# The first batch's per-token maxima in groups of two hidden tiles instead of four, and three tiny range steps with two tensor operands

## The chip, the core and the metric

The kernel runs on one core of one Trainium2 chip. The metric is the device time of one execution in microseconds. The time before is the median of three runs. A separate execution was profiled: its span runs from the first to the last instruction of the program, and its own device time stands beside it in the table below.

## What is computed

`x` is (4, 1024, 512), `up_w` is (4096, 512), `down_w` is (512, 2048). Cut to what matters:

```python
scale = cond @ norm_w.T + 1.0
h = x * (scale[:, None, :] * rsqrt(mean(x * x) + EPS))
val, gate = split(h @ up_w.T, 2)          # 2048 + 2048 columns
h = val * gelu(gate)
s = 127.0 / max(|h| over the 2048 columns of a token)
hq = clip(round(h * s)) / s               # act_quant
y = hq @ weight_quant(down_w).T           # weights -1, 0, 1
out = y + x
```

The change touches two things in it. One is the maximum of |h| over the 2048 columns of each token, for the first of the four batches. The other is a step that the kernel adds for its own sake: each row of `up_w` is brought to a common range with a power of two before it is split in two float16 parts.

## The kernel before

**Tiling.** There are four batches of 1024 tokens. The 2048 hidden columns are 16 tiles of 128, numbered `j`, and each tile has the tokens in two halves of 512, called `h`. A finished tile of h (128 columns in the partitions, 2 x 512 tokens) lies in one slot of the ring `H`, which has 18 slots. In the first batch slots from 8 on also hold weights and staging until the tiles need them.

**The first batch.** `first_batch(j)` runs for j = 3 to 15 in an order written out by hand; nothing is scheduled by a planner there. For each j TensorE (PE) runs `plain_half(j, 0)` and `plain_half(j, 1)`: 12 matmuls for the gate into `pg` and 12 for the value into `pv`, of 512 tokens each (L588). ScalarE (ACT) applies gelu (L612), and VectorE (DVE) multiplies (L616), which writes the tile into its slot and frees the PSUM bank of `pv`. There are two such banks (tag "E"), so the value matmuls of one half wait for the L616 of two halves before.

Between the two halves every engine also prepares later work, and each takes its work in program order:

- *Weights of tile j+3.* `w_range` (called at the start of j) is four or five tiny DVE steps after one reduction: the largest value of a row (L279), its power of two (`pow2_floor`, L149), the scale factor (L285), the reciprocal (L288), and `w_gain` (L294). All but L279 work on a 128 x 2 tile. `w_scale` (ACT, L306) multiplies the weights, `w_rows` splits them in two parts (ACT L330, then DVE L331), and a transposing DMA (L332) puts them into place for PE.
- *Sums of weights for the later batches.* GpSimd (POOL) forms `s_sums` (L364 to L367) and `s_low` (L380), ACT `s_high` (L376), and SyncE (SP) writes them to DRAM.
- *Tokens of the second batch.* For j = 6, 8, 10, 12 DVE scales a group of tokens (`Tokens.scale`, L517), POOL forms four sums (L528 to L531), and in the following odd j ACT (L552) and DVE (L556) split them and SP transposes them (L559).
- *The largest value of each token.* `pair_max` reduces |h| over some slots. For the first group it writes the running maximum directly (L702); for each later one it reduces into a scratch tile `gm` (L707) and takes the maximum of the two (L709). The calls in the first batch are listed by j in the dictionary `LARGEST`; they stand right after `plain_half(j, 0)`, so the multiplication L616 of the second half and the token scaling L517 stand behind them on DVE. `D_SUM` and `TOKENS` are similar lists.

The pair of slots 14 and 15 is left for the start of the second batch. In batches two to four `pair_max` already takes two slots a call.

**Later batches.** From the second batch on `slot(g)` runs seven products of six matmuls per tile (L573) on sums of the weights and tokens, and the quantized product with `down_w` is spread over them. The two `Filler` queues decide there where DVE and ACT steps go. The code of those batches is not in the diff.

**Startup.** For j = 0 and 1 `w_range` runs before the first products, for j = 0 in two calls of 128 x 1 each. POOL scales (L308), PE transposes (L316), ACT and DVE split.

Of the kernel before, what the change touches and what calls it, by code (L numbers as in the profile page):

```python
# [8 lines left out]
F32 = mybir.dt.float32  # L9
# [3 lines left out]
I32 = mybir.dt.int32  # L13
AF = mybir.ActivationFunctionType
ALU = mybir.AluOpType
# [3 lines left out]
P = 128  # L19
EXPONENT = 0x7F800000  # L20
# [5 lines left out]
W_UP = 2.0**12  # L26
# [24 lines left out]
def glu_quant_kernel(  # L51
# [10 lines left out]
    PE, ACT, DVE, POOL, SP = nc.tensor, nc.scalar, nc.vector, nc.gpsimd, nc.sync  # L62
# [7 lines left out]
    NJ = FF // P  # L70
# [4 lines left out]
    cpool = ctx.enter_context(tc.tile_pool(name="const", bufs=1))  # L75
# [4 lines left out]
    ident = cpool.tile([P, P], F32, name="ident")  # L80
    neghalf = cpool.tile([P, 4], F32, name="neghalf")
    DVE.memset(neghalf, -0.5)
    unmagic = cpool.tile([P, 1], F32, name="unmagic")
    DVE.memset(unmagic, -MAGIC)
    one = cpool.tile([P, 1], F32, name="one")
# [38 lines left out]
    def m_view(b, h):  # L124
        return R[:, b % 2, M_AT + TOK * h : M_AT + TOK * (h + 1)]
# [16 lines left out]
    def h_slots(g, n=1):  # L142
        s = g % NSLOT
        return H[:, s : s + n]

    def pow2_floor(t):

        ti = t.bitcast(I32)
        DVE.tensor_scalar(ti, ti, EXPONENT, None, ALU.bitwise_and)  # L149

    def bank(tag, bufs, shape=None, name=None):
        return psum.tile(shape or [P, TOK], F32, name=name or tag, tag=tag, bufs=bufs)
# [6 lines left out]
    dx = cpool.tile([P, B], F32, name="dx")  # L159
# [58 lines left out]
    def cond_spread(dg, b0, b1, tag):  # L218
        n = b1 - b0
        pd = bank(tag, {"po": 3}.get(tag, 2), [P, B], f"pd_{b0}")[:, :n]  # L220
        PE.matmul(pd, ones[:n, :], dg, start=True, stop=True)
        return pd

    def cond_undo(pd, b0, b1):
        DVE.reciprocal(ux[:, b0:b1], pd)
        if b0 == 0:
            DVE.tensor_scalar(scT[:, :, 0], scT[:, :, 0], ux[:, 0:1], None, ALU.mult)
        DVE.tensor_copy(dx[:, b0:b1], pd)

    def cond_rows():  # L230

        pr = po_bank("pr", [NK * B, P])
        PE.transpose(pr, scT.rearrange("p k b -> p (k b)"), ident)
        rows = sm.tile([NK * B, P], F32, name="rows", bufs=1)
        DVE.tensor_copy(rows, pr)
        SP.dma_start(out=rows_dram, in_=rows)
# [14 lines left out]
    sw = cpool.tile([P, NJ, 2], F32, name="sw")  # L251
    sg0 = sm.tile([P, NJ, 2], F32, name="sg_0", tag="sg")
# [16 lines left out]
    def w_load(j, ts=(1, 0)):  # L269
        if j > 2:  # L270
            SP.dma_start(out=wn(j), in_=up_v[j])
            return
        for t in ts:
            SP.dma_start(out=wn(j)[:, t], in_=up_v[j][:, t])

    def w_largest(j, t0=0, t1=2):
        t = slice(t0, t1)
        am = sm.tile([P, 2], F32, name=f"wam_{j}_{t0}", tag="wam")[:, t]
        DVE.tensor_reduce(am, wn(j)[:, t], AX.X, ALU.max, apply_absolute_value=True)  # L279
        return am  # L280

    def w_factor(j, am, t0=0, t1=2):
        t = slice(t0, t1)
        pow2_floor(am)
        DVE.tensor_scalar(sw[:, j, t], am, 2.0**-100, 1.0 / W_UP, ALU.max, ALU.mult)  # L285
        if j not in iv:
            iv[j] = sm.tile([P, 2], F32, name=f"iv_{j}", tag="iv", bufs=3)
        DVE.reciprocal(iv[j][:, t], sw[:, j, t])  # L288

    def w_range(j, t0=0, t1=2):  # L290
        w_factor(j, w_largest(j, t0, t1), t0, t1)

    def w_gain(j):
        DVE.tensor_scalar(sg0[:, j, :], sw[:, j, :], dx[:, 0:1], None, ALU.mult)  # L294

# [3 lines left out]
    def w_scale(j, ts=(1, 0), eng=None):  # L301
        eng = eng or (ACT if j >= ROWS else POOL)
        for t in ts:
            w, r = wn(j)[:, t], iv[j][:, t : t + 1]
            if eng is ACT:
                ACT.activation(w, w, AF.Copy, scale=r)  # L306
            else:
                eng.tensor_scalar(w, w, r, 1.0, ALU.mult, ALU.mult)  # L308
# [49 lines left out]
    def s_sums(j):  # L358
        if j >= ROWS:
            v = wn(j).rearrange("p t (n f) -> p t n f", n=2)  # L360
            a11, a12, a21, a22 = v[:, 1, 0], v[:, 1, 1], v[:, 0, 0], v[:, 0, 1]
        else:
            a11, a12, a21, a22 = (wf(j)[:, n] for n in range(4))
        POOL.tensor_tensor(sf[:, 0], a21, a22, ALU.add)  # L364
        POOL.tensor_tensor(sf[:, 2], a11, a21, ALU.subtract)
        POOL.tensor_tensor(sf[:, 1], sf[:, 0], a11, ALU.subtract)
        POOL.tensor_tensor(sf[:, 3], a12, sf[:, 1], ALU.subtract)  # L367
# [6 lines left out]
    def s_high(j):  # L374
        for s, f in s_parts(j):
            ACT.copy(s[:, :, 0], f)  # L376
# [60 lines left out]
    def d_total():  # L437
        part = sm.tile([P, 1], F32, name="wpart", bufs=1)
        DVE.tensor_reduce(part, wsum, AX.X, ALU.add)
        return part  # L440
# [7 lines left out]
    def d_round(n):  # L448

        dn = d_part(n)  # L450
        ACT.activation(dn, dn, AF.Copy, scale=wsc, bias=MAGIC)
# [156 lines left out]
    def plain_half(j, h, between=nothing):  # L608
        pg = bank(*(("A", 2) if h or j == 1 else ("B", 1)), name=f"pg_{j}_{h}")
        plain(j, 1, h, pg)  # L610
        t1 = wpool.tile([P, TOK], F32, name=f"g_{j}_{h}", tag="t1")
        ACT.activation(t1, pg, AF.Gelu, scale=gain(j, 1))  # L612
        between()
        pv = bank("E", 2, name=f"pv_{j}_{h}")
        plain(j, 0, h, pv)
        DVE.scalar_tensor_tensor(h_half(j, h), pv, gain(j, 0), t1, ALU.mult, ALU.mult)  # L616
# [77 lines left out]
        z()  # L694


    def pair_max(b, i, h, pairs=1):

        v = h_slots(b * NJ + 2 * i, 2 * pairs)[:, :, h].rearrange("p j t -> p t j")
        m = m_view(b, h)  # L700
        if i == 0:
            return [lambda: DVE.tensor_reduce(m, v, AX.X, ALU.max, apply_absolute_value=True)]  # L702
        gm = []

        def largest():
            gm.append(wpool.tile([P, TOK], F32, name=f"gm_{b}_{i}_{h}", tag="gm", bufs=1))
            DVE.tensor_reduce(gm[0], v, AX.X, ALU.max, apply_absolute_value=True)  # L707

        return [largest, lambda: DVE.tensor_tensor(m, m, gm[0], ALU.max)]  # L709
# [260 lines left out]
    am = w_largest(0, 1, 2)  # L970
# [25 lines left out]
    def second_part():  # L996
# [12 lines left out]
    D_MEAN = 4  # L1009
    TOKENS = {6: 0, 8: 1, 10: 2, 12: 3}  # L1010
    LARGEST = {
        4: (0, 0, 2), 5: (0, 1, 2), 8: (2, 0, 2), 10: (2, 1, 2), 12: (4, 0, 2), 13: (4, 1, 2),
        14: (6, 0, 1), 15: (6, 1, 1),
    }
    toks = {}

    def next_tokens(j):

        if j in TOKENS:
            toks[j] = toks[j + 1] = Tokens(1, TOKENS[j])  # L1020
            toks[j].load()

    def s_all(j):
        s_high(j)
        s_low(j, POOL)
        s_spill(j)

    def first_batch(j, sc):

        if j + 2 <= LATE:  # L1030
            w_load(j + 4)
        if j >= 4:
            next_tokens(j + 2)
        t = toks.get(j)
        odd = t is not None and j not in TOKENS
        n = j + 2
        rows = LATE <= n < NJ
        if j + 1 < LATE:
            s_sums(j + 1)
        elif rows:  # L1040
            s_sums(n)
        if j + 3 < NJ:
            w_range(j + 3)
            w_gain(j + 3)
        if j == D_MEAN:
            part = d_total()
        plain_half(j, 0)
        if j == 3:
            pd = cond_spread(dg, 1, B, "po")
            cond_undo(pd, 1, B)  # L1050
            cond_rows()
        if j in LARGEST:
            for f in pair_max(0, *LARGEST[j]):
                f()
        if n < LATE:
            w_scale(n)
            w_rows(n)
        if j + 1 < LATE:
            s_all(j + 1)
        if t and not odd:  # L1060
            t.norm()
        for m in D_ROUND.get(j, ()):
            d_round(m)
            d_put(m)
        if t and not odd:
            t.scale(sc)
            t.sums()
        if j + 2 > LATE and j + 5 < NJ:
            w_load(j + 5)
        if odd:  # L1070
            t.high()
            t.low(DVE)
        if odd:
            t.turn()
        plain_half(j, 1)
        if j == D_MEAN:
            d_mean(part)
        own = rows and j + 1 >= LATE
        if own:
            s_high(n)  # L1080
            s_low(n, POOL)
        if LATE <= j + 3 < NJ:
            w_scale(j + 3)
            w_rows(j + 3)
        if own:
            s_spill(n)
        elif rows:
            s_sums(n)
            s_all(n)
            w_load(j + 5)  # L1090
        for n in D_SUM.get(j, ()):
            d_sum(n)
        if j in (NJ - 3, NJ - 1):
            s_load_x(NJ + (j - NJ + 3) // 2)
            s_load_y(NJ + (j - NJ + 3) // 2)
# [174 lines left out]
    for b in range(1, B):  # L1270
        dve, act = Filler(), Filler()
        gains(b)
        am = am_tile(b - 1)
        dq = state[b - 1] = sm.tile([P, 2 * NA], F32, name=f"dq_{b}", tag="dq")
        last_pair = NJ // 2 - 1
        for h in range(2):
            add_pair(
                dve, act, b - 1, last_pair, h, (0, "xz"[h]),
                lambda now, h=h: token_max(b - 1, h, am),
# [9 lines left out]
        pairs = {}  # L1289
# [111 lines left out]
    b = B - 1  # L1401
    am = am_tile(b)
# [158 lines left out]
```

## Time and profile before

| | us |
|---|---|
| median of 3 runs | 734.88 |
| the three runs | 734.56, 734.88, 737.32 |
| the profiled execution | 733.24 |
| its span | 731.4 |
| PE busy in the span | 720.9 |
| DVE busy | 587.2 |
| ACT busy | 396.1 |
| POOL busy | 195.8 |

The granted TensorE clock is 1.00 throughout. A matmul of 512 columns starts every 0.216 us where PE is not held up, so 12 of them take 2.59 us; the rows of the timeline show 2.75 us for 12, because the last one's own duration (0.379 us) overlaps the next. A gap of PE is therefore read from the starts: the start of a group minus the start of the one before, less 2.59 us. The page's idle times are smaller than these gaps by some 0.16 us each.

### The profile page before, as it was taken

The numbers are of one execution on the slowest core, as the hardware profiler recorded it, in microseconds if no ns is written. First come the engines' busy times: TensorE is split into PE (matmuls) and PEld (weight loads), VectorE is DVE, ScalarE is ACT, GpSimd is POOL, SyncE is SP. The second block draws the span as 40 slices with busy tenths as digits, with TensorE's granted clock in tenths as the row PEclk, the third lists the DMA queues.
The fourth block names the chain that finished last, engine by engine and source line by source line (L and its number), as shares of the span: only waits on it lengthen the run. The fifth ranks groups of instructions, "written<-read, shape, count | busy, mean of one in ns | idle before, by whom it ended". The sixth has DMA issues, their size and how long they took to land.

```text
span 731.4 us, 10126 instructions
## 1 busy us (share of the span) xinstructions
PE 720.9 (99%) x3661; PEld 358.9 (49%) x3661; DVE 587.2 (80%) x805; ACT 396.1 (54%) x629; POOL 195.8 (27%) x207
## 2 busy tenths in 40 slices
PE   7999999999999999999999999999999999999998
PEld 3544444444444446655444445665444444445744
DVE  6977889887498899797689887787678888755897
ACT  5868875872236675444335676543433665332274
POOL 1379886666200032450010030461020000000100
PEclk9999999999999999999999999999999999999999
DMA  6759998987544554886735646756934545452253
GB/s 233 252 165 307 291 286 233 254 199 180 165 94 106 134 121 147 191 164 172 194 100 102 130 101 173 187 146 165 226 98 106 91 100 115 103 103 90 87 189 115
DMA packets 203982, 117.30 MB, mean 160 GB/s; under 512 B 165382, under 2 KB 174487, under 8 KB 203932
## 3 DMA queue, kind: packets, MB, share of 16 engines
q1 hardware_dynamic: 203642, 116.33, 62.3%
q8 instruction: 28, 0.46, 0.3%
q10 hardware_dynamic: 290, 0.33, 0.2%
q14 instruction: 22, 0.18, 0.1%
HBM read 54.22 MB, written 23.09 MB: 106 GB/s over the span
## 4 chain that ended last, share of the span: by engine, by line
PE 87%; DVE 4%; POOL 4%; DMA 2%; ACT 1%; issue 1%; SPq 0%; POOLq 0%; DVEq 0%; ACTq 0%
PE A L573 34%; PE E L573 17%; PE B L573 8%; PE po L844 8%; PE pg L588 6%; PE pv L588 6%; PE po_end L793 4%; DVE gm L707 1%; PE po L793 1%; DMA H<-in_x_dram 1%; POOL xt L529 1%; DMA SXY<-H 1%; POOL H L367 1%; PE po_B L844 0%; POOL R L380 0%
## 5 line engine op out<-in xcount | busy, mean ns | idle before, releaser
L573 PEld LDWEIGHTS <-SXY 128*128 128x128 f16 x2016 | 197.3, 98 | 232.3 <-issue 0.6
L573 PE MATMUL A<-R,SXY 128*128 128x512 f16 x1152 | 266.3, 379 | 0.0
L573 PE MATMUL E<-R,SXY 128*128 128x512 f16 x576 | 140.0, 379 | 0.1
L671 DVE SCALAR_TENSOR_TENSOR H<-A,sg,t 128x512 f32<-128x512 f32 x48 | 36.0, 750 | 73.3 <-PE A L573 73.1
L588 PEld LDWEIGHTS <-SXY 128*128 128x128 f16 x486 | 47.4, 98 | 59.0 <-issue 1.7
L765 DVE TENSOR_TENSOR H<-H,am 128x1024 f32<-128x1024 f32 x64 | 76.2, 1216 | 0.0
L723 POOL PARTITION_ALL_REDUCE am<-R x8 | 14.3, 1793 | 230.4 <-DVE R L709 230.4
L684 ACT ACTIVATE t<-t,sg 128x512 f32<-128x512 f32 x48 | 34.6, 721 | 70.3 <-DVE t L681 70.2
L707 DVE TENSOR_REDUCE gm<-H 128x512 f32<-128x1024 f32 (+1 forms) x50 | 71.6, 1433 | 0.8
L573 PE MATMUL B<-R,SXY 128*128 128x512 f16 x288 | 70.0, 379 | 0.0
L588 PE MATMUL pg<-R,SXY 128*128 128x512 f16 x252 | 57.8, 379 | 0.3 <-DMA SXY<-H 0.3
L844 PE MATMUL po<-wd,R 128*128 128x256 fp8e4 (+1 forms) x448 | 56.8, 275 | 0.0
L588 PE MATMUL pv<-R,SXY 128*128 128x512 f16 x234 | 54.4, 379 | 1.1 <-DVE H L616 1.0
L844 PEld LDWEIGHTS <-R 128*128 128x128 bf16 (+1 forms) x480 | 47.0, 98 | 12.8
L668 ACT ACTIVATE t<-B,sg 128x512 f32<-128x512 f32 x48 | 33.0, 687 | 36.5 <-PE B L573 36.5
L477 POOL TENSOR_SCALAR ssq<-ssq 128x2 f32<-128x2 f32 x12 | 3.6, 298 | 176.8 <-ACT xt L507 124.1
L651 ACT COPY t<-A 128x512 f32<-128x512 f32 x48 | 27.9, 582 | 39.5 <-PE A L573 39.2
L659 ACT COPY B<-A 128x512 f32<-128x512 f32 x48 | 27.4, 572 | 39.0 <-PE A L573 38.6
L773 ACT ACTIVATE H<-H 128x1024 f32<-128x1024 f32 x38 | 39.9, 1050 | 14.1 <-DVE H L765 14.1
L663 ACT COPY v<-E 128x512 f32<-128x512 f32 x48 | 28.1, 585 | 31.3 <-PE E L573 27.8
L690 DVE SCALAR_TENSOR_TENSOR H<-v,sg,t 128x512 f32<-128x512 f32 x48 | 36.6, 762 | 7.4 <-ACT t L684 7.4
L777 ACT ACTIVATE R<-H 128x1024 bf16<-128x1024 f32 x38 | 40.1, 1055 | 0.8
(205 smaller groups left out, 978.3 us busy)
## 6 DMA issues: line engine op xcount, KB each, us to landing
SXY<-s_dram SPq DMA_DIRECT2D x57, 256.0 KB, 3.0
s_dram<-SXY SPq DMA_DIRECT2D x18, 384.0 KB, 3.0
H<-in_L_cond_up_w_dram SPq DMA_DIRECT2D x13, 512.0 KB, 5.1
SXY<-s_dram SPq DMA_DIRECT2D x39, 128.0 KB, 3.1
xr<-in_x_dram SPq DMA_DIRECT2D x19, 256.0 KB, 3.3
out_dram<-xr SPq DMA_DIRECT2D x19, 256.0 KB, 2.6
H<-in_x_dram SPq DMA_DIRECT2D x8, 512.0 KB, 8.0
R<-in_L_cond_down_w_dram SPq DMA_DIRECT2D x8, 512.0 KB, 6.9
```

Of the source, the lines that this page charges most:

```text
L573: PE.matmul(o, s[:, w, k, :], tv[:, :, c, l, k, :], start=start and n == 0, stop=stop and n == len(TERMS) - 1, skip_group_check=True,)
L588: PE.matmul(ps, a[k // 2][:, w, k % 2, :], XP[:, l, k, h * TOK : (h + 1) * TOK], start=n == 0, stop=n == len(terms) - 1,)
L668: ACT.activation(cur["t1"], pb, AF.Gelu, scale=gain(g, 1))
L671: DVE.scalar_tensor_tensor(h_half(g - 1, 0), prev["A"], gain(g - 1, 0), prev["t1"], ALU.mult, ALU.mult)
L684: ACT.activation(prev["t2"], prev["t2"], AF.Gelu, scale=gain(g - 1, 1))
L690: DVE.scalar_tensor_tensor(h_half(g - 1, 1), prev["v"], gain(g - 1, 0), prev["t2"], ALU.mult, ALU.mult)
L707: DVE.tensor_reduce(gm[0], v, AX.X, ALU.max, apply_absolute_value=True)
L765: DVE.tensor_tensor(v, v, r.to_broadcast([P, 2, TOK]), ALU.mult)
L773: ACT.activation(v, v, AF.Copy, bias=MAGIC)
L777: ACT.activation(q, by_tile(v), AF.Copy, bias=-MAGIC)
L793: PE.matmul(po.rearrange("p (y c o) -> p y c o", c=2, o=P), q[:, a, h, j], wd8[:, :, j // n, j % n, :, y0:y1].rearrange("p c o y -> p y c o"),
L844: PE.matmul(po, w[:, j], m, start=start and j == 0, stop=stop and j == n - 1, skip_group_check=True,)
```

## The change

In the first batch `pair_max` loses its parameter for two pairs at once, and every call takes two slots. Before, there were six calls over four slots (j = 4, 5, 8, 10, 12, 13) and two over two slots (j = 14, 15), each for one half of the tokens. After, there are fourteen calls over two slots, two in each of j = 4, 5, 8, 10, 12, 14 and 15, one for each half; j = 13 has none.

Three small steps get two tensor operands in place of one tensor and a constant or a scalar per partition: the bitwise AND of `pow2_floor` with a constant tile `emask`, the factor of `w_factor` with a constant tile `undo_up`, and `w_gain` with `dx` broadcast to two columns. Two memsets of 128 x 2 fill the constant tiles at the start. The order of all other instructions on every engine stays as it was.

```diff
+    emask = cpool.tile([P, 2], I32, name="emask")
+    DVE.memset(emask, EXPONENT)
+    undo_up = cpool.tile([P, 2], F32, name="undo_up")
+    DVE.memset(undo_up, 1.0 / W_UP)
...
     def pow2_floor(t):
         ti = t.bitcast(I32)
-        DVE.tensor_scalar(ti, ti, EXPONENT, None, ALU.bitwise_and)
+        m = emask[: t.shape[0], : t.shape[-1]]
+        DVE.tensor_tensor(ti, ti, m, ALU.bitwise_and)
...
     def w_factor(j, am, t0=0, t1=2):
-        DVE.tensor_scalar(sw[:, j, t], am, 2.0**-100, 1.0 / W_UP, ALU.max, ALU.mult)
+        DVE.scalar_tensor_tensor(
+            sw[:, j, t], am, 2.0**-100, undo_up[:, t], ALU.max, ALU.mult
+        )
...
     def w_gain(j):
-        DVE.tensor_scalar(sg0[:, j, :], sw[:, j, :], dx[:, 0:1], None, ALU.mult)
+        DVE.tensor_tensor(sg0[:, j, :], sw[:, j, :], dx[:, 0:1].to_broadcast([P, 2]), ALU.mult)
...
-    def pair_max(b, i, h, pairs=1):
+    def pair_max(b, i, h):
-        v = h_slots(b * NJ + 2 * i, 2 * pairs)[:, :, h].rearrange("p j t -> p t j")
+        v = h_slots(b * NJ + 2 * i, 2)[:, :, h].rearrange("p j t -> p t j")
...
     LARGEST = {
-        4: (0, 0, 2), 5: (0, 1, 2), 8: (2, 0, 2), 10: (2, 1, 2), 12: (4, 0, 2), 13: (4, 1, 2),
-        14: (6, 0, 1), 15: (6, 1, 1),
+        4: ((0, 0), (0, 1)), 5: ((1, 0), (1, 1)), 8: ((2, 0), (2, 1)), 10: ((3, 0), (3, 1)),
+        12: ((4, 0), (4, 1)), 14: ((5, 0), (5, 1)), 15: ((6, 0), (6, 1)),
     }
...
-        if j in LARGEST:
-            for f in pair_max(0, *LARGEST[j]):
+        for i, h in LARGEST.get(j, ()):
+            for f in pair_max(0, i, h):
                 f()
```

## The prediction

> **What bounds the kernel now.** I read the page first. TensorE (PE) is busy almost throughout, so an engine that gets faster elsewhere pays only where it ends a gap of PE.
>
> ```profile
> PE 720.9 (99%) x3661; PEld 358.9 (49%) x3661; DVE 587.2 (80%) x805; ACT 396.1 (54%) x629; POOL 195.8 (27%) x207
> ```
>
> Next I went through PE's own timeline and took every place where two matmuls start more than 0.30 us apart. Most of the loss is startup before 18 us (13.76 us busy of 18) and the tail. Behind 60 us, and before the second batch starts at 188.4, only three gaps remain. Two of them are in these rows (start, duration):
>
> ```profile
> 155.15 2.75 PE L588 MATMUL pg<-R,SXY 128*128 128x512 f16 x12
> 158.00 2.75 PE L588 MATMUL pv<-R,SXY 128*128 128x512 f16 x12
> 160.59 2.75 PE L588 MATMUL pg<-R,SXY 128*128 128x512 f16 x12
> 164.39 2.75 PE L588 MATMUL pv<-R,SXY 128*128 128x512 f16 x12 [1.05 <-DVE H L616]
> ```
>
> Twelve matmuls are 2.59 us of starts. So 158.00 comes 0.26 late, 164.39 comes 1.21 late, and in the same way 175.49 (behind a group that started at 172.16) comes 0.74 late: 2.21 us in all. Each is a pv group that waits for VectorE's (DVE's) L616 of two halves before to free its bank: those L616 end at 157.95, 164.33 and 175.4. From 188.4 on PE runs without a gap but for 0.66 us at 324 and two of 0.2 us, in code that the diff leaves alone.
>
> Then the chain of waits, from 85 to 195 us, says why DVE is late there (start, duration):
>
> ```profile
> 115.54 1.42 DVE xa L517 x2
> ...
> 130.28 1.23 DVE H L331
> ...
> 134.59 3.67 DVE gm L707
> ...
> 138.89 1.42 DVE xn L517 x2
> ```
>
> Until 111 us this chain is PE's own matmuls. After it, it is a loop through the other engines, once in two tiles: DVE scales tokens (L517), GpSimd (POOL) does L528 to L367, ScalarE (ACT) L306 and L330, DVE L331, the small steps, L616, the large L707, and L517 again. L517 starts at 115.54, 138.89 and 162.26: a period of 23.35 us, where PE needs 8 x 2.59 = 20.72. The loop loses 2.63 us to PE each time, uses up DVE's lead, and then PE stops.
>
> **The change part by part: the maxima.** The durations, from the groups by line and shape (busy us, mean ns):
>
> ```profile
> L707 DVE TENSOR_REDUCE gm<-H 128x512 f32<-128x1024 f32 x46 | 56.6, 1231 | 0.8
> L709 DVE TENSOR_TENSOR R<-R,gm 128x512 f32<-128x512 f32 x50 | 38.1, 762 | 1.1
> ...
> L707 DVE TENSOR_REDUCE gm<-H 128x512 f32<-128x2048 f32 x4 | 15.0, 3752 | 0.0
> ...
> L294 DVE TENSOR_SCALAR sg<-sw,dx 128x2 f32<-128x2 f32 x16 | 9.1, 566 | 0.0
> ...
> L285 DVE TENSOR_SCALAR sw<-wam 128x2 f32<-128x2 f32 x15 | 7.8, 518 | 0.5
> ```
>
> Four slots cost 3.75 us, three times the 1.23 of two, not twice. By j, with 0.69 for an undisturbed L709: j = 4 goes from 3.77 to 2.46; j = 5 from 3.78 to 3.84; j = 8, 10 and 12 each from 4.44 to 3.84; j = 13 from 4.93 (3.77 + 1.16) to nothing; j = 14 and 15 each from 1.92 to 3.84. DVE in all loses some 4.2 us of work.
>
> What counts is where it lies. The maxima of j = 8, 10 and 12 stand in the loop, ahead of L517: 0.6 less each. POOL sits idle for 5.7 us ahead of each L528 there, so the second L709 is undisturbed. At j = 8 the chain also shows a DMA that ends at 115.23, only 0.31 before L517; if that binds, j = 8 gives 0.3 instead. Sum ahead of the L616 that ends at 164.33: 1.5 to 1.8. PE without its first gap wants that bank at 160.33 + 2.59 = 162.92; the L616 will end at 162.5 to 162.8. The L616 that ends at 157.95 comes 0.9 to 1.2 earlier, and is wanted at 157.74. Both gaps go (1.47 us), the second with only 0.1 to 0.4 to spare. Then j = 13 has no maximum. DVE there waits for ACT's L552 (167.66, 1.04), which stands behind the loop's POOL and so comes at 165.9 to 166.2; L556 (1.75) and L616 (0.74) behind it end near 169.7, and PE wants that bank at 162.92 + 4 x 2.59 = 173.28. The third gap goes too: 0.74.
>
> What gets longer, and its cover: at j = 14 and 15 the L616 of the second half stands behind 1.92 us more. In the trace DVE waits for PE there for 0.41, 4.39 and 2.58 us (rows at 178.37, 183.51, 188.71), and pv of the next half is two groups off. At j = 5 the two L709 run beside POOL and may take up to 1.75 each, the largest that L709 shows; behind them DVE waits 1.67 us for a DMA (89.23) anyway. Cost nothing; without that cover, 1 to 2 us would be lost. Part sum: -2.2 us, bounded by -1.2 (L616 at 164.33 gains only half) and -2.2, all there is.
>
> **The small steps.** L149, L285 and L294 at 128 x 2 take 0.17, 0.17 and 0.21 us when alone and 0.24, 0.52 and 0.57 on average. The excess is 15 x 0.07 + 15 x 0.35 + 16 x 0.36 = 12 us, and it is waiting for POOL: L294 of 144.41 takes 1.49, to 145.90, while POOL's L380 runs from 144.23 to 145.87. Do steps with two tensors wait less? Here are two rows of an existing one, L709:
>
> ```profile
> 169.83 0.73 POOL L364 TENSOR_TENSOR H<-H 128x256 f32<-128x256 f32 x1
> 169.94 1.16 DVE L709 TENSOR_TENSOR R<-R,gm 128x512 f32<-128x512 f32 x1
> ```
>
> It needs 0.69 and takes 1.16. L556 of 128x1024 takes 1.74 beside POOL and 1.22 without. So two tensors in SBUF wait for POOL also. I take the wait as unchanged: 0. The base cost falls little: a two-tensor step of 128 x 4 at 9.99 takes 0.16. Bounds: no wait at all saves 12 us of DVE, of which PE can only use the 0.49 gap at 50.88 (there L149 at 41.72 takes 0.70 ahead of the transfer that PE waits for); or each step waits for one POOL operation, 0.7 us, which makes a rival below.
>
> [...]
>
> **Startup.** At j = 0 the steps are 128 x 1, and L149 at 10.98 takes 0.15 although POOL's L929 runs from 10.73 to 11.63. With two tensors it may wait until 11.63, 0.6 us. POOL itself is not free for its next step L308 before 11.62, and PE's L316, which needs that, starts at 12.93, when 16 transposes end; L308 (0.70) would end near 12.9. So most is covered. I take +0.1, between 0 and +0.7 (one L308 more in front of ACT's L938). Two memsets add 0.06 us in front of DVE's first wait for PE and lie beside the load of x, which ends at 7.98: nothing.
>
> **Sum.** -2.2 + 0.0 + 0.1 = -2.1 us. The profiled execution would go from 733.24 (span 731.4 and 1.84 around it) to 731.1. It is 1.64 below the median, and the three runs spread by 2.8; carried to the median: 734.88 - 2.1 = 732.8.
>
> **The rivals.** *More is won:* the steps no longer wait for POOL, and the gap at 50.88 goes too: -2.2 - 0.49 = -2.7, 732.2. For it: the small row at 9.99. Against it: L709 and L556 above. *The bank is still late:* the DMA at 115.23 or a POOL wait in the loop leaves the 164.39 gap half in place: -2.2 + 1.0 = -1.2, and 733.7. For it: the spare is 0.1 to 0.4 us. *Slower:* L149, L285 and L294 of even j stand in the loop. They wait 0.58 us there now (L285 at 132.87, 0.75); if all three waited 0.7, a round would cost 1.5 more and save 0.6. It decides from 0.6 more per round on. Three rounds of +0.9 add 2.7 to the first two gaps; the third goes (-0.74), startup costs 0.7: +2.7, 737.6 (and past 739 where a step meets the 1.64 of L380 and not 0.7). For it: two-tensor rows wait, and at 10.98 one-column steps do not. Against it: L149 starts when POOL has just finished (132.66 against 132.78), and 128 x 2 steps already wait.
>
> **How the numbers follow.** The forecast gets 0.62, more won 0.12, the bank still late 0.10, slower 0.16. The range runs from 731.0 (the 2.7 won, and 1.2 for the spread of the runs) to 736.0, which leaves out the upper half of the slower rival. About 0.5% (3.7 us) is what a measurement of this kernel can tell from no change. A gain beyond it needs more than all gaps named, so mainly the spread or something unseen: 0.16. Slower by that much is the upper part of the slower rival: 0.10. Within it: 0.74.
>
> **What would show it.** Right: L707 and L702 only at 1.23 us; L517 near 138.0 and 160.6; PE's three gaps gone and the second batch starting near 186.2; L285 and L294 still with rows of 0.7 and more. Wrong: a PE group behind L616 that still comes late between 155 and 180, small steps of 0.16 throughout, or PE's L316 later than 13.0.

## The result, and the profile after

The changed kernel takes 731.85 us (median of 7 runs, 730.43 to 732.46) against 734.88 (7 runs of the kernel before, 733.38 to 737.32): a ratio of 0.9954, 95% interval 0.9939 to 0.9970. The profiled executions differ by 2.8 us (spans 731.4 and 728.6, own times 733.24 and 730.43). Taken once more beside other kernels, the ratio is 0.9967 (0.9952 to 0.9981). The prediction was 732.8.

In the changed file the lines behind L149 move by 5 to 7: L149 is L154 now, L285 is L290, L288 is L295, L294 is L301, L331 is L338, L367 is L374, L517 is L524, L588 is L595, L616 is L623, L702 is L709, L707 is L714.

The page's busy line of the changed kernel:

```profile
PE 719.9 (99%) x3661; PEld 358.8 (49%) x3661; DVE 581.2 (80%) x819; ACT 396.3 (54%) x629; POOL 196.1 (27%) x207
```

DVE has 14 instructions more and 6.0 us less to do. PE does the same work as before; what it lost was in gaps. Its timeline over the stretch that had them (start, duration):

```profile
157.12 2.75 PE L595 MATMUL pv<-R,SXY 128*128 128x512 f16 x12
159.71 2.75 PE L595 MATMUL pg<-R,SXY 128*128 128x512 f16 x12
162.29 2.75 PE L595 MATMUL pv<-R,SXY 128*128 128x512 f16 x12
...
172.66 2.75 PE L595 MATMUL pv<-R 128*128 128x512 f16 x12
```

Each group starts 2.59 us behind the one before it, and 172.66 is four more groups on: the gaps of 0.26, 1.21 and 0.74 us are gone. The chain of waits, from 85 to 195 us, is now PE's own matmuls from one end to the other; where before it left PE at 111 us for the loop, it reads

```profile
113.25 2.59 PE pg L595 x12
115.84 2.59 PE pv L595 x12
118.43 2.59 PE pg L595 x12
```

The loop is still there, but shorter than what PE can bear. DVE and one POOL instruction in a round of it, from the timeline:

```profile
114.13 1.41 DVE L524 SCALAR_TENSOR_TENSOR xa<-xa,rs,sc 128x512 f32<-128x512 f32 x2
...
128.87 1.23 DVE L338 TENSOR_TENSOR H<-H 128x1024 f16<-128x1024 f32 x1 [2.71 <-ACT H L337]
131.26 0.16 DVE L154 TENSOR_TENSOR wam<-wam,emask 128x2 int32<-128x2 int32 x1
131.46 0.16 DVE L290 SCALAR_TENSOR_TENSOR sw<-wam,undo_up 128x2 f32<-128x2 f32 x1
131.46 0.75 POOL L374 TENSOR_TENSOR H<-H 128x256 f32<-128x256 f32 x1
131.74 0.50 DVE L301 TENSOR_TENSOR sg<-sw,dx 128x2 f32<-128x2 f32 x1
132.82 1.22 DVE L714 TENSOR_REDUCE gm<-H 128x512 f32<-128x1024 f32 x1
134.80 1.24 DVE L714 TENSOR_REDUCE gm<-H 128x512 f32<-128x1024 f32 x1
136.68 1.41 DVE L524 SCALAR_TENSOR_TENSOR xn<-xn,rs,sc 128x512 f32<-128x512 f32 x2
```

L524 starts at 114.13, 136.68 and, one round on, 159.58: rounds of 22.55 and 22.90 where L517 had 23.35 and 23.37. Two rows of 1.22 and 1.24 stand where one of 3.67 stood. The groups by line and shape say the same for the whole program (busy us, mean ns):

```profile
L714 DVE TENSOR_REDUCE gm<-H 128x512 f32<-128x1024 f32 x56 | 69.0, 1232 | 1.0
L709 DVE TENSOR_REDUCE R<-H 128x512 f32<-128x1024 f32 x8 | 9.5, 1228 | 0.0
L301 DVE TENSOR_TENSOR sg<-sw,dx 128x2 f32<-128x2 f32 x16 | 8.8, 552 | 0.0
L290 DVE SCALAR_TENSOR_TENSOR sw<-wam,undo_up 128x2 f32<-128x2 f32 x15 | 4.9, 326 | 0.5
```

No row of 2048 elements is left. L301 costs what L294 cost (566 ns), L290 less than L285 (518 ns).

### The profile page after: what moved, and what is told of

Same layout as the page of the kernel before. It is cut to its first block, busy times and chain, and to the rows that moved or that the text cites. A ratio compares the mean times of both kernels' runs of the same rounds, so it can differ in the third digit from the quotient of the medians.

```text
span 728.6 us, 10140 instructions
## 1 busy us (share of the span) xinstructions
PE 719.9 (99%) x3661; PEld 358.8 (49%) x3661; DVE 581.2 (80%) x819; ACT 396.3 (54%) x629; POOL 196.1 (27%) x207
## 3 DMA queue, kind: packets, MB, share of 16 engines
HBM read 54.22 MB, written 23.09 MB: 106 GB/s over the span
## 4 chain that ended last, share of the span: by engine, by line
PE 96%; DVE 1%; DMA 1%; ACT 0%; issue 0%; SPq 0%; DVEq 0%
PE A L580 34%; PE E L580 17%; PE pg L595 10%; PE pv L595 10%; PE B L580 9%; PE po L851 8%; PE po_end L800 4%; PE po L800 1%; DMA H<-in_x_dram 1%; DMA SXY<-H 1%; PE po_B L851 0%; PE ptx L941 0%; PE pv L638 0%; DVE R L949 0%; PE pw L323 0%; PE pg L638 0%
## 5 line engine op out<-in xcount | busy, mean ns | idle before, releaser
L595 PEld LDWEIGHTS <-SXY 128*128 128x128 f16 x486 | 47.5, 98 | 57.4 <-DMA SXY<-H 0.8
L714 DVE TENSOR_REDUCE gm<-H 128x512 f32<-128x1024 f32 x56 | 69.0, 1232 | 1.0
L595 PE MATMUL pg<-R,SXY 128*128 128x512 f16 x252 | 57.8, 379 | 0.3 <-DMA SXY<-H 0.3
L595 PE MATMUL pv<-R,SXY 128*128 128x512 f16 x234 | 54.4, 379 | 0.0
L716 DVE TENSOR_TENSOR R<-R,gm 128x512 f32<-128x512 f32 x56 | 41.9, 749 | 1.3
```

Source lines behind the costliest of these rows:

```text
L595: PE.matmul(ps, a[k // 2][:, w, k % 2, :], XP[:, l, k, h * TOK : (h + 1) * TOK], start=n == 0, stop=n == len(terms) - 1,)
```

## Where the time goes: one stretch, and the rest

One stretch of PE's timeline holds the loop and little else: from the transpose of the token factors near 56 us to the 1301st matmul, in the second batch. It takes 224.18 to 224.19 us in five of the profiles below, those without a gap from 60 us to the second batch. What a kernel spends beyond 224.18 there is what the loop costs PE. Before has 226.39, after 224.18: 2.21 of the 2.81 us between the two spans. Another 0.63 lies ahead of the stretch, and 0.48 of that is the first transposes of the tokens, which begin at 11.12 and at 10.64 (the load of `x` lands at 7.98 and 7.51). From the 1301st matmul on, all kernels agree within 0.07 us (but for the one that appends work at its end).

Ahead of 56 us the executions of one and the same kernel differ. The runs of after have spans from 728.6 to 730.7. Its second profile has a span of 731.8 and the loop at 224.19: all of the 3.1 us between its two profiles lie ahead of the loop. PE, busy time and granted clock (PEclk) from 14 to 20 us, in the first profile and in the second (columns: window, its length, PE, PEld, DVE, ACT, POOL, PEclk, DMA share, GB/s):

```profile
14.00:20.00 6.00, 5.77 (x33) 3.15 (x32) 5.89 (x14) 5.30 (x11) 0.69 (x1) 1.00 0.52 161
```

```profile
14.00:20.00 6.00, 5.32 (x19) 2.33 (x17) 3.29 (x9) 3.21 (x7) 1.06 (x2) 0.55 0.13 37
```

In the second PE does 19 matmuls where the first does 33, at a granted clock of 0.55. So a span tells little, and the experiments are read by the excess in the stretch beside the medians. The rounds are those from tile 8 to 10 and from 10 to 12:

| kernel | ratio to before (95%) | excess in the stretch, us | rounds of the loop, us |
|---|---|---|---|
| before, two profiles | 0.9995 (0.9983 to 1.0006) for the second | 2.21, 2.90 | 23.35, 23.37; 23.76, 23.76 |
| pairs alone | 0.9972 (0.9962 to 0.9982) | 1.08 | 22.85, 22.85 |
| steps alone | 0.9980 (0.9970 to 0.9989) | 2.81 | 23.41, 23.06 |
| steps alone, again | 0.9979 (0.9968 to 0.9989) | 1.86 | 23.09, 23.06 |
| steps alone, third profile | | 1.84 | 23.10, 23.07 |
| both (after), two profiles | 0.9954, 0.9967 | 0.00, 0.01 | 22.55, 22.90; 22.88, 22.89 |
| after, with reductions appended at its end | | 0.82 | 22.88, 22.56 |
| after without the maxima | 0.9962 (0.9948 to 0.9975) | 0.00 | 19.22, 20.24 |
| after, as long as before | 0.9998 (0.9987 to 1.0009) | 1.51 | 23.61, 23.28 |
| before, fours in odd tiles | 0.9975 (0.9961 to 0.9988) | 0.01 | 21.44, 21.41 |
| before, steps by column | 0.9989 (0.9978 to 1.0000) | 2.94 | 23.22, 23.22 |
| after, steps by column | 0.9955 (0.9943 to 0.9968) | 0.00 | 22.71, 22.70 |

The rounds alone don't give the excess; where the loop starts counts as much. Count both from the transpose of the token factors: tile 6's token scaling starts at 35.5 to 36.9 us, three rounds later comes tile 12's, and in each of the nine profiles with an excess PE's lateness behind the second gap (ahead of the third) is what tile 12's start exceeds 104.31 us by, within 0.02 us (before 105.79 and 1.47, pairs alone 105.39 and 1.08). In the five without gaps it starts at 104.05 or earlier.

## The experiments

**The kernel before, once more.** No edit.

> The kernel before, unchanged, as a second profile of it. It tells what of the 2.8 us between the two profiled spans belongs to the change. Theory one (the three PE gaps of 0.26, 1.21 and 0.74 us are the whole effect, the other 0.5 us is when the first load of x happens to land): ratio 1.000, the three gaps again within 0.1 us of their sizes, the first transpose of PE anywhere between 10.6 and 11.2 us. Theory two (the startup became faster by the change): the first transpose again at 11.1 us.

The median is 733.46 us, the same as the 733.91 of the kernel before beside it. The first transposes begin at 10.49 us here, so their early start after the change (10.64) was not the change's doing. But the gaps are not within 0.1 us of their sizes: they are 0.93, 1.21 and 0.77 us (2.90 beyond 224.18) where the first profile had 2.21, with rounds of 23.76. The 0.4 us in each round come from POOL in the odd tile. The first profile, and below it this one (start, duration):

```profile
123.11 0.72 POOL L364 TENSOR_TENSOR H<-H 128x256 f32<-128x256 f32 x1
123.11 2.12 DVE L556 TENSOR_TENSOR nx<-xa,nx 128x512 f16<-128x512 f32 x2
```

```profile
122.33 1.27 POOL L364 TENSOR_TENSOR H<-H 128x256 f32<-128x256 f32 x1
122.34 1.54 DVE L556 TENSOR_TENSOR nx<-xa,nx 128x512 f16<-128x512 f32 x2
```

The two start within 10 ns of each other, POOL's first in both. In one execution DVE's L556 waits, in the other POOL's L364 does (the starts don't tell why), and the loop runs through POOL: its L367 of that tile ends 0.2 us later in the round and the L380 behind it starts 0.4 later. So differences of 0.7 us in the loop between two single profiles come without any change of the kernel.

**The pairs alone.** The new `pair_max` and `LARGEST`, with the three steps as before.

> Only the maxima by pairs; the small steps stay with one tensor and a constant. Loop theory: the round from token scaling to token scaling falls from 23.35 to about 22.75 us, all three gaps of PE between 155 and 180 us go or leave at most 0.2, time 2.0 to 2.2 us below the kernel before (ratio 0.997). Rival (the small steps gave a part of it: their waits fell from 12 to about 9.5 us): at least one gap of 0.3 us or more stays, and the time is only 1.0 to 1.6 us below.

731.93 us, 2.0 less than before. The rounds are 22.85 us, 0.5 shorter than the 23.35 and 23.37 of the first profile of before, where DVE and POOL meet in the same order. The third gap is gone, and 0.40 and 0.68 us of the first two stay: neither expectation holds whole, since the time is that of the loop theory and the gaps are those of the rival. The loop started late in this profile (tile 6's token scaling at 36.45, in before at 35.67). By the sum above, with the earlier start about 0.3 us of the gaps would have been left (an estimate from these rows). So the maxima bring most of the gain in the loop; what the steps add is not to be read from this one profile.

**The steps alone.** The three two-tensor steps, with the maxima as before.

> Only the three small steps with two tensors; the maxima stay in fours. Loop theory: steps with two tensors in SBUF wait for GpSimd as the old ones did, the sum of the three lines at 128 x 2 stays at 17 to 21 us, and of the gaps at most 0.5 us goes; ratio 0.999 to 1.000. Rival: the steps alone shorten the round by 0.3 us or more, the gaps fall by 1 us or more and the ratio is 0.998.

732.43 us, 1.5 less: the ratio of the rival, but not its gaps. They are 0.10, 0.75, 1.20 and 0.77, nearly as long as those of the second profile of before. So the same kernel ran again, twice.

> The kernel before with the three two-tensor steps and nothing else, taken once more, since its one profile showed all the gaps of before (0.10, 0.75, 1.20 and 0.77, sum 2.8 us) while its median was 1.5 us below the kernel before. Theory 'the profile was an untypical entry': the loop gains about 0.3 us per round by the order of DVE and GpSimd, the gaps in this profile sum to 1.3 to 2.2 us, and the ratio is 0.998 to 0.999. Rival 'nothing won in the loop': the gaps sum to 2.2 to 2.9 again with rounds of 23.4, and the ratio is 0.9995 to 1.0005, so the first median was a shift of the startup.

> A third profile of the two-tensor steps alone, one look. Theory 'untypical entry': gaps of 1.3 to 2.2 us in sum. Rival 'nothing won in the loop': 2.2 to 2.9.

Both new profiles have gaps of 1.09 and 0.76 us and an excess of 1.86 and 1.84, and five of the six rounds in the three profiles measure 23.06 to 23.10. The ratio repeats at 0.9979. So the steps alone win 0.3 us in five of six rounds. In the stretch three profiles with 2.81, 1.86 and 1.84 stand against two of before with 2.21 and 2.90, which is too few to say how much of the 1.5 us lies there; the rest was not found.

Where the 0.3 comes from is a race between DVE and POOL. The same place in the kernel before, from its timeline:

```profile
132.66 0.17 DVE L149 TENSOR_SCALAR wam<-wam 128x2 int32<-128x2 int32 x1
132.86 0.73 POOL L367 TENSOR_TENSOR H<-H 128x256 f32<-128x256 f32 x1
132.87 0.75 DVE L285 TENSOR_SCALAR sw<-wam 128x2 f32<-128x2 f32 x1
...
133.73 0.21 DVE L294 TENSOR_SCALAR sg<-sw,dx 128x2 f32<-128x2 f32 x1
```

L285 starts some 10 ns behind POOL's L367 and takes 0.75, until POOL is done; L294 then takes 0.21. In the rows of after above, L290 starts in the same 10 ns as POOL's L374 and takes 0.16; L301 runs into it, late, and takes 0.50. The two steps together take 0.96 us before and 0.66 after. The same pair of rows stands in the third profile of the steps alone (L290 0.16 at 155.80, L301 0.49 at 156.08). The traces agree throughout: between 95 and 165 us, in the profiles with 128 x 2 steps, the old L285 starts 5 to 17 ns behind a POOL row 18 times and waits each time; the new L290 does so 7 to 11 ns behind 10 times and waits, and 29 times it starts between 6 ns ahead and 5 ns behind and does not. That the 10 ns come from L154 taking 0.16 where L149 took 0.17 fits, but no run sets them alone.

The odd tile has such a meeting too, and there a step that doesn't wait makes the round longer. The one round of the six that is not shorter, 23.41 us in the first profile of the steps alone, is the one in which L290 did not wait in the odd tile:

```profile
120.72 0.16 DVE L290 SCALAR_TENSOR_TENSOR sw<-wam,undo_up 128x2 f32<-128x2 f32 x1
121.00 0.49 DVE L301 TENSOR_TENSOR sg<-sw,dx 128x2 f32<-128x2 f32 x1
122.08 2.36 DVE L563 TENSOR_TENSOR nx<-xa,nx 128x512 f16<-128x512 f32 x2
123.05 1.12 POOL L387 TENSOR_TENSOR R<-H,R 128x256 f16<-128x256 f32 x1
```

Counted from the token scaling DVE comes to L563 1.6 us sooner, and POOL's L387, of 0.67 in the other five rounds, takes 1.12; the sums behind it come later, and the round is 0.3 us longer. The rounds of the changed kernel fit: 22.55 and 22.56 where DVE waits in the odd tile, 22.88 to 22.90 where it doesn't. No run sets the order in the odd tile by itself.

**No maxima.** The changed kernel without the maxima of slots 2 to 13 in the first batch; that work is left out.

```diff
-    LARGEST = { 4: ((0, 0), (0, 1)), 5: ..., 15: ((6, 0), (6, 1)) }
+    LARGEST = {4: ((0, 0), (0, 1))}
```

> The change, with all maxima of the first batch after the first pair left out (slots 2 to 13 are not taken into the maxima). It is the ceiling of what cheaper maxima can give. Gap theory: PE has no gap left there in the changed kernel, so 22 us less work of VectorE give nothing more: the same time as the changed kernel, 0.995 to 0.997 of before. Rival (VectorE's load counts beyond the gaps, through contention or later work): 1 us or more below the changed kernel.

731.26 us, ratio 0.9962: no faster than the changed kernel. DVE does some 23 us less there and PE gains nothing; in an execution whose stretch has no gap, what maxima still cost after the change is hidden.

**The changed kernel, once more.** No edit.

> The changed kernel once more, beside the next three on one chip. Loop theory: no gap of PE between 150 and 185 us, 2.2 us below the kernel before plus at most 0.5 for the steps' order against GpSimd: ratio 0.9965 to 0.997. If the steps gain something of their own that no gap shows (steps alone measured 0.998 with all three gaps in the one profile of it), pairs and steps add up to about 0.995.

732.32 us; the stretch is again without a gap, with rounds of 22.88. Its profile is the one with the slow startup shown above.

**The same length as before.** The changed kernel, with one more maximum of two (the one of 0.69 us) in tiles 8, 10 and 12.

```diff
             for f in pair_max(0, i, h):
                 f()
+            if h and j in (8, 10, 12):
+                f()
```

> The changed kernel with one more maximum of running maximum and scratch (0.69 us, the same values again) behind the pairs of tiles 8, 10 and 12, so that they are as long as the fours were. Loop theory: the round is 23.2 to 23.6 us again, the first two gaps come back with 0.7 to 1.5 us together, the third (0.74) does not; 0.7 to 1.5 us above the changed kernel. Rival (the empty tile 13 is what matters): no gap comes back.

The gain is gone: 733.97 us, ratio 0.9998, 1.65 us above the changed kernel beside it. The rounds are back at 23.61 and 23.28, and PE's timeline shows a gap where it was:

```profile
160.95 2.75 PE L595 MATMUL pg<-R,SXY 128*128 128x512 f16 x12
164.95 2.75 PE L595 MATMUL pv<-R,SXY 128*128 128x512 f16 x12 [1.25 <-DVE H L623]
```

4.00 less 2.59 is 1.41 us late, and the one before 0.10. The third gap does not return: tile 13 is still empty. So the 0.6 us in each round closes the first two gaps, and the move out of tile 13 closes the third without it.

**The fours elsewhere.** The kernel before, with its fours as long as they were, but in tiles that have no token scaling.

```diff
-        4: (0, 0, 2), 5: (0, 1, 2), 8: (2, 0, 2), 10: (2, 1, 2), 12: (4, 0, 2), 13: (4, 1, 2),
-        14: (6, 0, 1), 15: (6, 1, 1),
+        4: ((0, 0, 2),), 5: ((0, 1, 2),), 9: ((2, 0, 2),), 11: ((2, 1, 2),), 13: ((4, 0, 2),),
+        14: ((4, 1, 2),), 15: ((6, 0, 1), (6, 1, 1)),
```

> The kernel before with its maxima still over four slots, but out of the loop: those of tiles 8, 10, 12 and 13 move to the odd tiles 9, 11, 13 and to 14, behind which VectorE sits idle for 2.7 us once in a round. VectorE does the same work. Place theory (what counts is what stands ahead of the token scaling): the round falls to PE's own 20.7 to 21.5 us, the three gaps go or leave at most 0.4, ratio 0.997. Price theory (what counts is the 4.2 us less of VectorE's work): the three gaps stay, ratio 0.9995.

All three gaps go: the excess is 0.01 us, the rounds are 21.44 and 21.41, the ratio is 0.9975. Its group by shape and PE's timeline:

```profile
L707 DVE TENSOR_REDUCE gm<-H 128x512 f32<-128x2048 f32 x4 | 14.9, 3736 | 0.0
```

```profile
161.43 2.75 PE L588 MATMUL pg<-R,SXY 128*128 128x512 f16 x12
164.02 2.75 PE L588 MATMUL pv<-R,SXY 128*128 128x512 f16 x12
```

The four reductions cost 3.74 us each, as before, and PE does not notice, although one of them still stands in tile 13. Out of the place ahead of L517, and with the lead that this leaves, their price costs the kernel nothing.

**The steps by column.** Each of the three steps as two `tensor_scalar` of one column, once on the changed kernel and once on the kernel before; the short diff of the first of the three:

```diff
-        DVE.tensor_scalar(ti, ti, EXPONENT, None, ALU.bitwise_and)
+        for c in range(t.shape[-1]):
+            v = ti[:, c : c + 1]
+            DVE.tensor_scalar(v, v, EXPONENT, None, ALU.bitwise_and)
```

> The changed kernel with each of the three small steps as two tensor_scalar of one column (128 x 1), six instructions for three. The 128 x 1 steps of before at 10.98 us took 0.15 beside GpSimd. If one column with one tensor never waits: every step takes 0.14 to 0.17 us, the three lines together fall from 17 us to about 15, spread over twice the count with no row over 0.3, and the gap of 0.47 us at 50 us shrinks since the step at 41 us no longer waits 0.5; 0.3 to 0.5 us below the changed kernel, which is at the edge of what the runs can tell. Rival (they wait like the others): rows of 0.5 and more, no gain.

> The kernel before (maxima by fours, at the slots of before) with each of the three steps as two tensor_scalar of one column. Theory 'the rounds decide, wherever the time in them comes from': six one-column steps of at most 0.2 us each take the place of three that waited 0.6 us in a round beyond their own 0.5, so a round is 22.7 to 23.1 instead of 23.35 to 23.76 although the maxima by fours stay; the first two gaps shrink to 0.9 or less in sum, the gap at 50 us (0.49) goes, the third (0.74) stays, as the maximum of tile 13 does; about 1.5 us less, ratio 0.9975 to 0.9985. Rival 'the maxima alone decide': rounds of 23.3 or more, all three gaps of the loop stay at 2.2 or more, and only the 0.49 goes, ratio 0.999 to 1.000.

On the changed kernel: 730.87 us, ratio 0.9955. The three lines of code, one by one (duration in ns: smallest, median, largest):

```profile
L155 DVE TENSOR_SCALAR wam<-wam x32: 142/150/155, 11.0 to 155.1; 128x1 int32<-128x1 int32 x32
...
L292 DVE TENSOR_SCALAR sw<-wam x32: 144/153/154, 11.2 to 155.3; 128x1 f32<-128x1 f32 x32
...
L306 DVE TENSOR_SCALAR sg<-sw,dx x32: 193/202/206, 14.8 to 155.7; 128x1 f32<-128x1 f32 x32
```

None of the 96 waits for POOL; in the changed kernel L290 goes up to 1571 ns and L301 up to 1487, and the 128 x 2 steps of before go as high. The gap at 50 us that every kernel without this edit has (0.47 in after) is gone. The stretch has no excess to win, so that gap is all the gain behind the startup that its profile shows. Its median is 1.45 us below that of the changed kernel beside it, but the two intervals against before overlap (0.9943 to 0.9968, 0.9952 to 0.9981).

On the kernel before, my expectation was wrong. Its rounds are 23.22 us, not 22.7 to 23.1, and all three gaps stay, 2.94 in the stretch; only the 0.47 at 50 us goes, and the ratio of 0.9989 is that of the rival. In the even tile the six steps do save 0.44 us from the start of the first to the end of the last (1.27 us at 132.66 before, 0.84 at 134.08 here). What I left out is the odd tile. There the steps don't wait either, DVE reaches the work behind them sooner, POOL's second L388 takes 1.12 in place of 0.67 (L380), and the even tile's steps come 0.3 us later in the round. Of the 0.44 a round keeps 0.15.

**The price of a maximum.** The changed kernel with twenty more reductions appended at its end, two of each form, where DVE has nothing beside it.

> The changed kernel with maxima of other forms appended at its end, each twice, into a tile of their own, so that DVE runs them with nothing beside them but the last stores; its time as a whole says nothing. By the row of two slots (1024 elements in 1.23 us, 1.04 ns each with 0.16 us around) three slots would take 1.76 us, four 2.29, six 3.36, eight 4.43. Theory 'the fourth slot makes each element slower, whatever the distance': four elements for an output take 3.75 us also at half the distance, at a distance that is no power of two, and when they lie side by side; six and eight slots cost about 1.8 ns per element (5.6 and 7.3 us). Rival 'the distance of 4 KB is what is slow': four slots at another distance take about 2.3 us and only those at 4 KB take 3.75; two slots at 16 KB may then be slow too.

Six of the forms (512 outputs each but in one row; duration in ns: smallest, median, largest):

```profile
L1551 DVE TENSOR_REDUCE probe<-H x2: 1911/1912/1912, 729.8 to 731.7; 128x512 f32<-128x1536 f32 x2
...
L1551 DVE TENSOR_REDUCE probe<-H x2: 3619/3619/3619, 733.7 to 737.3; 128x512 f32<-128x2048 f32 x2
...
L1551 DVE TENSOR_REDUCE probe<-H x2: 7032/7032/7032, 751.8 to 758.8; 128x512 f32<-128x4096 f32 x2
...
L1551 DVE TENSOR_REDUCE probe<-H x2: 3619/3619/3619, 766.0 to 769.6; 128x512 f32<-128x2048 f32 x2
...
L1551 DVE TENSOR_REDUCE probe<-H x2: 1884/1884/1885, 780.6 to 782.5; 128x256 f32<-128x1024 f32 x2
L1551 DVE TENSOR_REDUCE probe<-H x2: 2286/2286/2286, 784.4 to 786.7; 128x512 f32<-128x2048 f32 x2
```

In order: three slots; four slots; eight slots; four at half the distance (2 KB); four slots into 256 outputs; four that lie side by side. Two slots take 1.23 us, at 4 KB and at 16 KB alike. Neither theory holds whole. The distance made no difference here: four at 2 KB, at 4 KB and at 4 KB + 32 bytes take 3.62 (3619, 3619 and 3618 ns). But that they lie apart does: four side by side take 2.29, what the row of two slots promises. With 0.16 us taken off (what DVE's reduction of 128 x 4 takes at 5.25 us in before), an element costs 1.04 ns with two slots, 1.14 with three, and 1.68 to 1.69 with four, six (5.32 us) and eight. Why the fourth makes the step was not found.

Up to the appended work this is the changed kernel with the same instructions in the same order, so its profile is a third one of the changed kernel, and its first batch has two gaps again, of 0.13 and 0.69 us:

```profile
155.20 2.75 PE L595 MATMUL pg<-R,SXY 128*128 128x512 f16 x12
157.91 2.75 PE L595 MATMUL pv<-R,SXY 128*128 128x512 f16 x12
160.50 2.75 PE L595 MATMUL pg<-R,SXY 128*128 128x512 f16 x12
163.78 2.75 PE L595 MATMUL pv<-R,SXY 128*128 128x512 f16 x12 [0.53 <-DVE H L623]
```

Its rounds are those of the second profile of after, but its loop starts 1.26 us later (tile 6's token scaling at 36.79 and 35.53). One reason stands in tile 5, where the maxima got longer:

```profile
83.79 2.05 DVE L716 TENSOR_TENSOR R<-R,gm 128x512 f32<-128x512 f32 x1
```

In after the same step takes 0.69 at 82.36, and DVE waits 1.14 us for a DMA behind the maxima of tile 5; here there is no wait left to cover it. (Late starts come with the fours too: 36.49 in the first profile of the steps alone, 36.87 in before with steps by column.) So the change doesn't close the gaps in every execution.

## Why the prediction was right

**What bounds the kernel: right.** The three gaps were DVE's, through the loop: without the extra work in the round (pairs alone) or with it moved out of the round (fours in odd tiles) they shrink or go; with it put back (same length) two of them return.

**The maxima, -2.2 us: right in place, and in size with some luck.** 0.6 us less per round was forecast, and the pairs alone show 0.5. But -2.2 is the sum of the gaps in one profile: the second profile of before has 2.90, pairs alone leave 1.08 us of excess, and the third profile of the changed kernel has 0.82. I took the start of the loop and the order in which DVE and POOL meet as fixed, and both move from one execution to the next by more than the spare. In the first profile of the changed kernel the L623 that stands where the late L616 stood (164.33) ends at 161.65, and PE wants the bank at 162.29: a spare of 0.64, where I gave 0.1 to 0.4. The longer j = 14 and 15 cost nothing, as said: the second batch starts without a gap. The longer j = 5 cost nothing in two of three profiles of the changed kernel; in the third its cover, the wait for a DMA, did not suffice.

**The small steps, 0: the term that was mis-sized.** Their waiting does stay, as I argued from L709 and L556. But the sum of the three at 128 x 2 fell from 20.4 us to 17.4 (16.0 to 19.2 in the other profiles with the new steps). I took "the wait is unchanged" for each step by itself and did not ask in which order DVE and POOL reach the place: a step that started between 6 ns ahead of POOL and 5 ns behind paid nothing (L290, 0.16 at 131.46), and its successor paid part (L301, 0.50), where the old L285 paid 0.75. That takes 0.3 us off a round in the even tile, and gives 0.3 back where it happens in the odd tile too. By medians the steps alone are worth 1.5 us (ratios of 0.9980 and 0.9979, both intervals below 1); how much of it lies in the loop stays open. With both parts there is less to win than their sum (2.0 + 1.5), since in no profile is the stretch shorter than 224.18.

What stayed is in the durations: with two tensors L290 takes up to 1571 ns in the changed kernel and L301 up to 1487, as L285 and L294 did before. What I left out is the order of the starts, and the rows at 131.46 and 132.87 show it: L290, in the same 10 ns as POOL's L374, takes 0.16; L285, some 10 ns behind POOL's L367, takes 0.75.

**Startup, +0.1: nothing.** L323 (L316 before) starts at 12.45, which is 1.81 us behind the first transposes, as before (11.12 and 12.93). The wait is there, but on another step than I named: the one-column L154 at 10.50 takes 0.15, the L290 at 10.69 takes 0.46, while POOL's L936 runs from 10.26 to 11.16. It is hidden, as forecast for most of it.

**The rivals.** *More is won* names a gain of about this size (2.7), but not by its mechanism: the steps still wait, and the gap at 50 us stays at 0.47. Steps by column show what that rival needed. *The bank is still late* is what the profile of the pairs alone and the third of the changed kernel show, by a late start of the loop, and not by the DMA that I named. Its price doesn't follow from its words: half of the gap of 1.21 is 0.6, not 1.0, so -1.6 and not -1.2. *Slower* did not come: in the round's rows at 131 only L301 waits (0.50), not all three steps. My reading that L149 starts when POOL has just finished was not what the numbers beside it say: 132.66 is 0.12 ahead of 132.78.

**The number.** -2.1 was forecast; the medians moved by 3.0 in the first comparison and the ratio of the second gives 2.4. The profiled pair differs by 2.8, of which 2.2 lies in the loop and 0.6 ahead of it. What the medians moved beyond the forecast is not explained: ahead of 56 us one and the same kernel moves by up to 3.1 us from one execution to the next, and no run tells whether the change has a part in it.

## What to carry to other kernels

Look for the chain that closes on itself and compare its period with what the bounding engine needs, and see whether the work lies in it: here 0.6 us less work in it made the round 0.5 shorter, and four maxima of 3.74 us, moved one tile further on, left an excess of 0.01. When that chain is a little longer than the engine's own period, gaps open only after the lead is used up, so a small cut per round can close all of them, and a second cut wins nothing more while the lead lasts (23 us less work of DVE here). The start of the loop moves between executions (tile 6's token scaling at 35.53 and 36.79 us behind the transpose of the token factors, with the same instructions), so a small spare is not safe. Where two engines make each other wait, work out which of them starts first before you price the wait, and which of the two the chain runs through: an engine off the chain that gets ahead can make the round longer (23.41 us here, where the other five had 23.06 to 23.10). Judge by a stretch of the bounding engine in more than one profile, not by one span.

## What the runs showed of the hardware

With 0.16 us taken off, a maximum over four, six or eight elements that lay apart cost 1.68 to 1.69 ns for each (3.62, 5.32 and 7.03 us for 512 outputs), over two 1.04 (1.23 us); four side by side cost 1.04 also (2.29 us). In the changed kernel with steps by column the one-column `tensor_scalar` steps never waited for GpSimd (96 steps, at most 206 ns), while in the changed kernel a one-column step with two tensors did (0.46 at 10.69 us; the one ahead of it, at 10.50, took 0.15 beside the same POOL row) and 128 x 2 steps of both kinds did (up to 1571 ns, L285 before and L290 after). Why the one-column `tensor_scalar` steps did not wait, no run shows.
